# First value products in two halves of 256 queries, and one head's exponentials part by part

## The chip, the cores and the metric

The kernel runs on one core of a Trainium2 chip. Its metric is the time of one execution on the device, in microseconds (us). A core has a matrix engine (PE; its weight loads are listed as PEld), a vector engine (DVE), a scalar engine (ACT), GpSimd (POOL) and a queue engine that issues DMAs (SP). Each engine works through its own queue in order; they wait for each other through semaphores. Products of PE land in PSUM, which is used here as banks of 128 rows by 512 float32 values.

## The reference

`x` has 32 sequences of 512 tokens with 256 channels: 16 heads of 16 channels. Two causal attentions share the queries; the second one's values are the errors of the first. Then come a layer norm and, for the first sequence's 512 tokens alone, 8 experts.

```python
qk = x @ W_attn + b_attn                      # q and k; the values v are x itself, by head
y = causal_attn(q, k, v)                      # softmax(q k^T / 4), keys up to the query's own
e = v[:, :, 1:, :] - y[:, :, :-1, :]
k2 = x[:, :-1] @ W_k2 + b_k2
y2 = causal_attn(q[:, :, 1:, :], k2, e)       # a row of zeros is put in front
x = layernorm(x + proj(y) + proj(y2))
...
x = layernorm(x + experts(x))                 # experts' part: the first 512 tokens
```

## The kernel before, in words

**Groups and steps.** Four heads make a group, so a sequence has 4 groups and the whole input has 128. `step(n)` (L689) works on several groups at different stages: the row maxima of group n, the scores and exponentials of group n-1, the first attention's values of group n-2 (`a = 0`, tile `v_pad`) and the second's (`a = 1`, tile `e_pad`). The kernel is one long pipeline of such steps.

**Slots.** A step has five slots, 0 to 4. `slot(n, u)` (L395) merges four streams of products into one order for PE: for each pair of heads the maxima (`maxima`, L271, products in L301, tile `sm`) and the scores (`scores`, L356, products in L372, tile `sc`). Pair 1 begins with its scores and ends with its maxima, pair 0 the other way round. So pair 1's scores are a slot's first scores. When the last product of a stream is written down, its follow-up is written too: `exponentials()` (L380) for scores, `largest()` for maxima, which DVE does (L325).

**Scores and exponentials.** A slot's scores of one pair fill two banks, one for each head (`hh` 0 and 1). The list `banks` (L348) says what stands in a bank. Slots 1 and 4 have one part of 512 columns. Slots 0 and 2 have two, 384 and 128 columns (keys of block 1, and of block 3 of the group before). Slot 3 has two of 256. Each part takes three products (`k` = 0, 1, 2; the last subtracts the row maxima). ACT turns a bank into exponentials with one instruction of 512 columns (L384), four a slot in the order pair 1 head 0, pair 1 head 1, pair 0 head 0, pair 0 head 1. POOL then blanks the keys that lie after the query (L388).

**Banks.** `bank()` gives out four PSUM banks in turn. So whatever is the next to take a bank after a slot's four score banks takes the bank of pair 1, head 0, and must wait until its exponentials are done.

**Between the slots.** After each slot PE does what `step` listed for it (`rest`): after slot 0 a projection half (`project`, L228, tile `pj`) and an output projection (`attended`, L551, `po`); after slot 1 the first attention's values; after slot 2 transposes (`normalize`, L504, `yt`) and a projection half; after slot 3 a projection half and queries 0 to 255 of the second attention's values; after slot 4 queries 256 to 511. In the steps of the experts their products (L640, L665) are put in as well.

**Values.** `values(n, a, lo, hi)` (L428) multiplies the exponentials of key blocks `j` into one bank, for queries `lo` to `hi`, four heads to each block, and ACT copies the bank to `avs` (L450). For `a = 0` it is called once, for all 512 queries: blocks 0, 2, 1, 3 with 512, 256, 384 and 128 queries, 16 products. `gather` (L461, L462) then sends `avs` by DMA.

**Who orders what.** The order on PE, SP, DVE and POOL is the order of the program; ACT's is left to the scheduler of the language.

Of the kernel before, what the change touches and what calls it, by code (L numbers as in the profile page):

```python
# [13 lines left out]
AF = mybir.ActivationFunctionType  # L14
# [3 lines left out]
P = 128  # L18
HD = 16
# [16 lines left out]
def half(ap):  # L36
    return ap.bitcast(F32R)
# [3 lines left out]
def block_kernel(  # L41
# [16 lines left out]
    nc = tc.nc  # L58
    B, T, C = x.shape
# [21 lines left out]
    def bank(name):  # L81
        return psum.tile([P, T], F32, tag="one", name=name, bufs=4)
# [134 lines left out]
    def prepare(n):  # L217
        b, g = divmod(n, NG)
        s = seqs[b]
        heads = slice(g * GH, (g + 1) * GH)  # L220
        nc.gpsimd.tensor_copy(of_group(v_pad, g), s["x"].rearrange("p n (h d) -> p n h d", d=HD)[:, :, heads])
# [134 lines left out]
    def scores(n, u, pair):  # L356
        parts = [p for p in banks[u] if 0 <= n - p[3] < n_all]
        if not parts:
            return [], lambda: None
        ps = [bank(f"sc{n}_{u}_{pair}_{hh}") for hh in range(NH2)]  # L360
        pt = work.tile([P, NH2, T], F32, tag=f"pt{u}", name=f"pt{n}_{u}_{pair}", bufs=2)
        todo = []


        def score(d, a, j, at, k, hh, rows):
            keys = minus[a][rows] if k == 2 else d["kk"][rows, a, j * P : (j + 1) * P]
            queries = d["q"][rows, k, j * P :] if k < 2 else d["m"][rows]
            to = ps[hh][:, at * P : at * P + T - j * P]
            if k == 2:
                queries = queries.rearrange("p (r i q) -> p i r q", r=GH, i=NB)[:, j:]  # L370
                to = to.rearrange("p (i r q) -> p i r q", r=GH, q=HS)
            nc.tensor.matmul(to, half(keys), half(queries), start=(k == 0), stop=(k == 2))  # L372

        for a, j, at, lag in parts:
            d = groups[n - lag]
            d["pt", a, j, pair] = pt[:, :, at * P : at * P + T - j * P]
            for k in range(3):
                todo.append((T - j * P, partial(score, d, a, j, at, k)))

        def exponentials():  # L380
            lo = parts[0][2] * P
            hi = parts[-1][2] * P + T - parts[-1][1] * P
            for hh in range(NH2):
                nc.scalar.activation(pt[:, hh, lo:hi], ps[hh][:, lo:hi], AF.Exp, scale=HD**-0.5)  # L384

            for a, j, at, _ in parts:
                diag = pt[:, :, at * P : (at + 1) * P]
                nc.gpsimd.affine_select(  # L388
                    diag, diag, pattern=[[0, NH2], [1, P]], compare_op=ALU.is_ge, fill=0.0, base=-a,
                    channel_multiplier=-1,  # L390
                )

        return todo, exponentials
# [34 lines left out]
    def values(n, a, lo=0, hi=T):  # L428
        b, g = divmod(n, NG)
        d = groups[n]  # L430
        vals = (v_pad, e_pad)[a]

        def first_of(g, h):
            return (g // 2 * GH + h) * WIDE + 2 * (g % 2)

        ps = bank(f"av{n}_{a}_{lo}")
        order = [j for j in ([0, 2, 1, 3] if a == 0 else [0, 1, 3, 2]) if j * P < hi]
        for j in order:
            first = max(lo, j * P)
            for h in range(GH):  # L440
                nc.tensor.matmul(  # L441
                    ps[HS * h : HS * (h + 1), first - lo : hi - lo],
                    vals[:, j, first_of(g, h) : first_of(g, h) + HS],
                    d["pt", a, j, h // NH2][:, h % NH2, first - j * P : hi - j * P],
                    start=(j == order[0]),
                    stop=(j == order[-1]),
                )
        if lo == 0:
            d["avs", a] = work.tile([P, T], F32, tag="avs", name=f"avs{n}_{a}")
        nc.scalar.copy(d["avs", a][:, lo:hi], ps[:, 0 : hi - lo])  # L450

# [76 lines left out]
    def second_norm(b, t):  # L528
        norm(t, f"b{b}")
        nc.sync.dma_start(out[b].rearrange("(n p) c -> p n c", p=P), t)  # L530
# [54 lines left out]
    def store(b):  # L585
        nc.sync.dma_start(out[b].rearrange("(n p) c -> p n c", p=P), seqs.pop(b)["h"])
# [102 lines left out]
    def step(n):  # L689
        ready = lambda k: 0 <= k < n_all  # L690
        rest = [[] for _ in units]
        b, r = divmod(n, NG)
        two, odd = divmod(n, 2)
        ahead, behind = two + 1, two - 2
        if ready(n):
            prepare(n)

        def add(gap, f, *args):
            rest[gap].append(partial(f, *args))

        if ready(n - 1):
            add(0, augment, n - 1)
        if ready(2 * ahead):
            if odd:
                add(0, project, ahead, 0, T // 2)
                add(0, spread, ahead, 1, 0)
                add(2, project, ahead, 2, 0, T // 2)
                add(3, project, ahead, 2, T // 2)
            else:
                add(0, project, ahead, 1, 0, T // 2)  # L710
                add(2, project, ahead, 1, T // 2)
                add(3, project, ahead, 0, 0, T // 2)
        if ready(2 * behind) and not odd:
            add(0, narrow, behind)
        if ready(2 * two) and two and not odd:
            add(0, spread, two, 0, 1)
        if ready(n - 2):
            soon = n > n_all
            add(0 if soon else 1, values, n - 2, 0)
            add(0 if soon else 1, gather, n - 2, 0)  # L720
            rest[1 if soon else 2].insert(0, partial(normalize, n - 2))
            add(3, values, n - 2, 1, 0, T // 2)
            add(4, values, n - 2, 1, T // 2)
        if ready(2 * ahead) and odd:
            add(1, spread, ahead, 1, 1)
            add(2, spread, ahead, 0, 0)
            add(4, spread, ahead, 2, 0)
        if ready(2 * behind) and not odd:
            add(2, inverse, behind)
            add(3, unload, behind)  # L730
            add(4, widen, behind)
            if n > n_all + 1:
                add(4, weigh, behind)
                add(4, unite, behind)
        if ready(2 * behind) and odd and n < n_all + 2:
            add(1, weigh, behind)
            add(3, unite, behind)
        if ready(2 * two) and two and not odd:
            add(1, spread, two, 2, 1)
        if ready(n):  # L740
            add(4, halve, n)
        if ready(n - 2):
            add(4, gather, n - 2, 1)
        if r == 1 and b + 1 < B:
            add(2, load, b + 1)
        if r == 3 and b + 1 < B:
            add(2, load_next, b + 1)

        for b in range(B):
            end = (b + 1) * NG - 1  # L750
            last = b == B - 1
            for i in range(NB):
                if n == (end + 4 if last else min(end + 5 + i, n_all)):
                    add(0, attended, b, i)
                    if 0 < b < B - 1:
                        add(1, scaled, b, i)
            if n == end + 2:
                add(2, load_residual, b)
            for part in range(2):
                if n == (end + 3 if last else min(end + 3 + 2 * part, n_all - 1)):  # L760
                    add(3, biased, b, part)
            if 0 < b < B - 1 and n == min(end + 9, n_all + 2):
                rest[1].append(lambda b=b: store(b))


        e = n - first_expert
        if e == -1:
            rest[4] += [route, turn_tokens, lambda: load_hidden(0), lambda: load_down(0)]
        if e == 0:
            rest[0].insert(0, biases)  # L770
        if 0 <= e < E:
            rest[3].insert(0, lambda: hidden(e, 0, 0))
            rest[4].insert(0, lambda: hidden(e, 0, 1))
        if 0 <= e - 1 < E:
            rest[0].insert(0, lambda: hidden(e - 1, 1, 0))
            rest[1].insert(0, lambda: hidden(e - 1, 1, 1))
            rest[2].insert(0, lambda: down(e - 1))
            if e < E:
                rest[1].append(lambda: load_hidden(e))
                rest[2].append(lambda: load_down(e))  # L780
        if e == E:
            rest[4].append(lambda: second_norm(0, moe["acc"]))
        for s in range(len(units)):
            slot(n, s)
            for f in rest[s]:
                f()
# [94 lines left out]
```

## Time and profile before

| what | value |
|---|---|
| median of 3 runs | 2552.66 us (2551.92 to 2559.37) |
| the profiled execution's own time | 2553.1 us |
| its span in the trace | 2551.4 us |
| DVE busy | 2034.4 us (80%) |
| POOL busy | 1751.4 us (69%) |
| exponentials on ACT (L384) | 2564 instructions |
| values of the first attention on PE (L441, `v_pad`) | 4096 records, two to a product |
| values of the second attention on PE (L441, `e_pad`) | 6144 records |
| copies `avs` on ACT (L450) | 128 of 512 columns, 256 of 256 columns |

The span runs from the first to the last instruction of the program; the execution's own time has a little around it. A line of the timeline view gives the start, the length, the engine, the source line and the operation; equal instructions that follow each other are merged, with their count. Square brackets hold the engine's idle time before it and who ended it. "x32" for products of float32 means 16 products of two records.

### The profile page before, as it was taken

What the parts mean: (1) busy time and instruction counts of PE and PEld (TensorE: products, weight loads), DVE (VectorE), ACT (ScalarE), POOL (GpSimd) and SP (SyncE); (2) the same over time, 40 slices, a digit from 0 to 9 for tenths busy, and PEclk for the clock granted to TensorE, in tenths of its full rate; (3) what the DMA queues carried; (4) which work ended last, traced back from release to release, by engine and by line L of the source; (5) the groups of instructions that cost most, each with busy time, mean ns of one, the idle gap of its engine ahead of it and who ended that gap; (6) DMA issues with size and microseconds to landing.
All of it is one profiled execution on the core that took longest, in us unless ns stands there. A gap on an engine that the chain in (4) does not pass through costs nothing. (4 is left out here: it accounts for less than half of the span.)

```text
span 2551.4 us, 87424 instructions
## 1 busy us (share of the span) xinstructions
PE 2416.2 (95%) x35080; PEld 1735.8 (68%) x35080; DVE 2034.4 (80%) x3227; ACT 1660.6 (65%) x3350; POOL 1751.4 (69%) x3254
## 2 busy tenths in 40 slices
PE   7999999999999999999999999999999999999995
PEld 4766666677667667677776777677766767777763
DVE  6878777788888878888887888888887888888881
ACT  2766444476666667676766767667666667767662
POOL 4655555577777767777776777677776777777774
PEclk7999999999999999999999999999999999999997
DMA  5445433354545445445554545445454545445431
GB/s 136 109 111 134 112 100 107 96 134 125 131 133 130 120 120 129 134 131 134 132 138 106 133 125 132 132 128 139 111 132 125 135 129 134 128 115 133 127 102 60
DMA packets 262660, 314.04 MB, mean 123 GB/s; under 512 B 83064, under 2 KB 152688, under 8 KB 262256
## 3 DMA queue, kind: packets, MB, share of 16 engines
q1 hardware_dynamic: 259824, 308.01, 45.7%
q8 instruction: 278, 4.55, 0.8%
q14 instruction: 126, 1.03, 0.1%
q10 hardware_dynamic: 2368, 0.42, 0.1%
q0 software_dynamic: 64, 0.02, 0.0%
HBM read 115.26 MB, written 25.17 MB: 55 GB/s over the span
## 5 line engine op out<-in xcount | busy, mean ns | idle before, releaser
L325 DVE TENSOR_REDUCE top<-sm 128x2 f32<-128x1024 f32 (+4 forms) x1802 | 1529.4, 901 | 314.2 <-PE sc L372 189.1
L384 ACT ACTIVATE pt<-sc 128x512 f32<-128x512 f32 (+1 forms) x2564 | 1323.2, 603 | 441.2 <-PE sc L372 412.9
L388 POOL TENSOR_SCALAR_AFFINE_SELECT pt<-pt 128x256 f32<-128x256 f32 x2048 | 793.0, 409 | 636.4 <-ACT pt L384 627.4
L301 PE MATMUL sm<-kk_t,q_t 32*128 32x512 f32 (+2 forms) x7168 | 1031.1, 379 | 22.5 <-DMA kk_t<-pk 9.7
L372 PE MATMUL sc<-q_t,kk_t 32*128 32x256 f32 (+3 forms) x8192 | 993.0, 336 | 6.1 <-ACT pk L240 4.3
L372 PEld LDWEIGHTS sc<-q_t,kk_t 32*128 32x128 f32 x8192 | 646.8, 184 | 202.3 <-ACT pt L384 87.8
L372 PE MATMUL sc<-m_t,minus 32*128 32x256 f32 (+3 forms) x4096 | 694.7, 319 | 0.3
L301 PEld LDWEIGHTS sm<-kk_t,q_t 32*128 32x128 f32 x7168 | 611.1, 190 | 32.8 <-issue 18.3
L228 PE MATMUL pj<-xT,wq_sb 128*128 128x256 f32 (+1 forms) x1524 | 437.9, 411 | 44.7 <-DMA xT<-in_xT 9.3
L372 PEld LDWEIGHTS sc<-m_t,minus 32*128 32x128 f32 x4096 | 433.9, 185 | 12.4 <-issue 1.3
L228 PEld LDWEIGHTS pj<-xT,wq_sb 128*128 128x128 f32 x1524 | 264.1, 192 | 131.7 <-ACT pt L384 81.3
L441 PE MATMUL av<-pt,e_pad 128*32 128x256 f32 (+1 forms) x6144 | 335.0, 352 | 14.3 <-POOL e_pad L513 6.3
L450 ACT COPY avs<-av 128x256 f32<-128x256 f32 (+1 forms) x384 | 170.3, 444 | 265.6 <-issue 169.4
L286 PE MATMUL sm<-hide,pick 32*128 32x256 bf16 (+1 forms) x2560 | 337.0, 258 | 0.0
L441 PE MATMUL av<-pt,v_pad 128*32 128x512 f32 (+3 forms) x4096 | 303.9, 436 | 19.9 <-ACT pt L384 19.2
L441 PEld LDWEIGHTS av<-pt,e_pad 128*32 128x32 f32 x6144 | 170.0, 110 | 164.4 <-issue 46.0
L240 ACT ACTIVATE pk<-pj,bp_qk 128x256 f32<-128x256 f32 (+1 forms) x381 | 185.8, 488 | 129.5 <-PE pj L228 90.0
L441 PEld LDWEIGHTS av<-pt,v_pad 128*32 128x32 f32 x4096 | 142.0, 110 | 187.0 <-issue 160.6
L246 POOL TENSOR_TENSOR pk<-pk,lead 128x512 fp32r<-128x512 f32 x192 | 244.8, 1275 | 16.6 <-ACT lead L245 0.8
L581 POOL TENSOR_SCALAR h<-h,mv,r 128x256 f32<-128x256 f32 x120 | 147.0, 1225 | 13.1
L551 PE MATMUL po<-wp_sb,ysT 128*128 128x256 f32 x512 | 135.3, 390 | 12.7 <-POOL ysT L497 12.3
L243 POOL CAST lead<-pk 128x512 fp32r<-128x512 f32 x189 | 115.4, 611 | 28.5 <-ACT pk L240 26.8
(84 smaller groups left out, 1559.3 us busy)
## 6 DMA issues: line engine op xcount, KB each, us to landing
q_t<-lead SPq DMA_DIRECT2D x256, 128.0 KB
q_t<-pk SPq DMA_DIRECT2D x256, 128.0 KB
kk_t<-lead SPq DMA_DIRECT2D x256, 128.0 KB
kk_t<-pk SPq DMA_DIRECT2D x256, 128.0 KB
num<-avs SPq DMA_DIRECT2D x256, 128.0 KB
r<-inv SPq DMA_DIRECT2D x128, 256.0 KB
xT<-in_xT SPq DMA_DIRECT2D x32, 512.0 KB
x<-in_x SPq DMA_DIRECT2D x32, 512.0 KB
```

Source lines behind the costliest of these rows:

```text
L228: nc.tensor.matmul(ps[:, 0 : hi - lo], wq_sb[:, m, c, part * P : (part + 1) * P], seqs[b]["xT"][:, c, lo:hi], start=(c == 0), stop=(c == N ...
L240: nc.scalar.activation(pk[:, lo:hi], ps[:, 0 : hi - lo], AF.Identity, bias=bp_qk[:, m, part : part + 1])
L246: nc.gpsimd.tensor_sub(half(pk), pk, lead)
L286: nc.tensor.matmul(ps[hh][:, 0 if alone else hh].rearrange("p (k c) -> p k c", c=P)[:, first::step], pick[rows], hide[rows, kinds[0] : kin ...
L301: nc.tensor.matmul(part(ps[hh], i, na, at)[:, 0 if alone else hh], half(d["q"][rows, k, i * P : (i + 1) * P]), half(d["kk"][rows, a : a + ...
L325: nc.vector.tensor_reduce(to, view, AX.X, ALU.max)
L372: nc.tensor.matmul(to, half(keys), half(queries), start=(k == 0), stop=(k == 2))
L384: nc.scalar.activation(pt[:, hh, lo:hi], ps[hh][:, lo:hi], AF.Exp, scale=HD**-0.5)
L388: nc.gpsimd.affine_select(diag, diag, pattern=[[0, NH2], [1, P]], compare_op=ALU.is_ge, fill=0.0, base=-a, channel_multiplier=-1,)
L441: nc.tensor.matmul(ps[HS * h : HS * (h + 1), first - lo : hi - lo], vals[:, j, first_of(g, h) : first_of(g, h) + HS], d["pt", a, j, h // N ...
L450: nc.scalar.copy(d["avs", a][:, lo:hi], ps[:, 0 : hi - lo])
L581: by.tensor_scalar(t[:, i], t[:, i], mv[:, 0:1], r, ALU.subtract, ALU.mult)
```

## The change

1. The first attention's values are made in two products of 256 queries in two banks, the later half (queries 256 to 511) first. The tile `avs` is made by whichever comes first. The later half takes blocks 0, 2, 1, 3 with 256, 256, 256 and 128 queries; the earlier half takes blocks 0 and 1 with 256 and 128. ACT copies each half by itself.
2. Where a bank of pair 1's scores, a slot's first, has two parts (slots 0, 2 and 3), the exponentials of head 0 are made with one instruction for each part. Head 1, pair 0, and slots 1 and 4 stay as they were.

```diff
         def exponentials():
-            lo = parts[0][2] * P
-            hi = parts[-1][2] * P + T - parts[-1][1] * P
+            runs = [(at * P, at * P + T - j * P) for _, j, at, _ in parts]
             for hh in range(NH2):
-                nc.scalar.activation(pt[:, hh, lo:hi], ps[hh][:, lo:hi], AF.Exp, scale=HD**-0.5)
+                for lo, hi in runs if pair and not hh else [(runs[0][0], runs[-1][1])]:
+                    nc.scalar.activation(pt[:, hh, lo:hi], ps[hh][:, lo:hi], AF.Exp, scale=HD**-0.5)
...
-        if lo == 0:
+        if ("avs", a) not in d:
             d["avs", a] = work.tile([P, T], F32, tag="avs", name=f"avs{n}_{a}")
         nc.scalar.copy(d["avs", a][:, lo:hi], ps[:, 0 : hi - lo])
...
             soon = n > n_all
-            add(0 if soon else 1, values, n - 2, 0)
+            for half_of in (T // 2, 0):
+                add(0 if soon else 1, values, n - 2, 0, half_of, half_of + T // 2)
             add(0 if soon else 1, gather, n - 2, 0)
```

## The prediction

> **What bounds the kernel now.** I read the page first, then the waits, then the timeline of one step, and then counted over all steps what the timeline showed in one. The page:
>
> ```profile
> span 2551.4 us, 87424 instructions
> PE 2416.2 (95%) x35080; PEld 1735.8 (68%) x35080; DVE 2034.4 (80%) x3227; ACT 1660.6 (65%) x3350; POOL 1751.4 (69%) x3254
> L384 ACT ACTIVATE pt<-sc 128x512 f32<-128x512 f32 (+1 forms) x2564 | 1323.2, 603 | 441.2 <-PE sc L372 412.9
> ```
>
> PE is busy 95%, but ACT, at 65%, sits on the same path: its exponentials wait 412.9 us for PE's scores. The waits view has the other direction:
>
> ```profile
> PEld sc L372 <- ACT pt L384: 87.8, 244, 0.4
> PEld pj L228 <- ACT pt L384: 81.3, 229, 1.4
> PEld av L441 <- ACT pt L384: 45.8, 120, 0.9
> ```
>
> The waits are short, but there is one in almost every slot. The timeline shows what sets their length. These are slots 0, 1, 2 and 4 of one step, each with ACT's exponentials and PE's next work:
>
> ```profile
> 1207.62 2.06 ACT L384 ACTIVATE pt<-sc 128x512 f32<-128x512 f32 x4 [0.68 <-PE sc L372]
> 1208.27 0.73 PEld L228 LDWEIGHTS pj<-xT,wq_sb 128*128 128x128 f32 x4 [0.30 <-ACT pt L384]
> ...
> 1211.24 2.06 ACT L384 ACTIVATE pt<-sc 128x512 f32<-128x512 f32 x4 [1.20 <-PE sc L372]
> 1211.98 2.36 PE L441 MATMUL av<-pt,v_pad 128*32 128x512 f32 x32 [0.15 <-ACT pt L384]
> 1214.28 0.44 PE L372 MATMUL sc<-q_t,kk_t 32*128 32x384 f32 x2
> 1214.45 0.59 ACT L450 COPY avs<-av 128x512 f32<-128x512 f32 x1 [1.14 <-issue]
> 1215.46 2.06 ACT L384 ACTIVATE pt<-sc 128x512 f32<-128x512 f32 x4 [0.43 <-POOL r L578]
> 1216.11 0.66 PE L504 MATMUL yt<-ident,avs 128*128 128x128 f32 x4
> ...
> 1222.32 2.06 ACT L384 ACTIVATE pt<-sc 128x512 f32<-128x512 f32 x4 [0.50 <-PE sc L372]
> 1222.97 1.72 PE L441 MATMUL av<-pt,e_pad 128*32 128x256 f32 x32
> ```
>
> From the start of the first exponential to PE's next work it is 0.65 us in slots 0, 2 and 4 (8.27 - 7.62, 16.11 - 15.46, 22.97 - 22.32): the 0.60 us of one exponential, and 0.05 us until PE goes on, since that work takes the bank of pair 1, head 0. Read record by record over the whole trace, PE's next piece starts within 0.08 us of such an end in 98 of 116 slots 0, 119 of 120 slots 2, 115 of 116 slots 3, and 27 more in the experts' steps: 359 places. So **the first exponential of each slot ends the slot**, and its length is paid in full. A normal step takes 18.2 us.
>
> In slot 1 the time is 0.74 us, 0.09 more, in 119 of 120 steps. There the first product of values has two waits, for its bank (ACT) and for blanked exponentials (POOL), and a separate wait instruction stands ahead of it (51 ns each in the trace, PE's queue, L441). Slot 4's values have one wait and none ahead.
>
> **Part 2, the exponentials.** In the changed program ACT gets 383 more exponentials; POOL's, DVE's and SP's orders are the same to the row. The first part's exponential waits for the same count of PE as the whole did before: the last product of the bank. The second waits for nothing, and only its end reports to PE. So **nothing starts earlier**, and the split is one more instruction ahead of each release. The row: slot 2's scores of the first part end at about 15.07, its whole bank at 15.35 and the exponential starts at 15.46, the later of the two.
>
> The Trainium skill says why the bank is the unit ("PSUM — Partial Sum Buffer", section "PSUM bank collisions raise a hardware error"): PE writing and ScalarE reading one bank at once collide even at different columns, so one guards by bank. It speaks against this change; without it the first parts could start 0.28 us earlier and the sum would be some 80 us lower.
>
> Price of one more instruction: from the rows by form, 512 columns take 0.603 us and 256 take 0.392 us, so 0.181 us is fixed; the copies (0.587 and 0.372 us) give 0.157.
>
> ```profile
> L384 ACT ACTIVATE pt<-sc 128x256 f32<-128x256 f32 x8 | 2.7, 392 | 3.2 <-PE sm L286 2.0 <-PE sm L301 0.9 <-PE sc L372 0.3
> L450 ACT COPY avs<-av 128x256 f32<-128x256 f32 x256 | 95.2, 372 | 102.4 <-PE av L441 73.4 <-ACT pk L240 21.3 <-issue 7.4
> L450 ACT COPY avs<-av 128x512 f32<-128x512 f32 x128 | 75.1, 587 | 163.2 <-issue 161.9 <-PE av L441 1.2
> ```
>
> Back to back they overlap: four take 2.06, so (2.06 - 0.60) / 3 = 0.487 us from start to start, 0.116 less than one alone. The split then costs 0.041 to 0.065 us; with no overlap 0.157 to 0.181. I take 0.055, since the second part has no wait at all, fewer than the pairs that the trace shows overlapping. 359 x 0.055 = **+19.7 us**; with no overlap at 0.167, +60. Behind the split stand the three other exponentials of the slot, 0.055 later; POOL and the next slot's scores wait for those, but the scores come over 2 us later.
>
> The skill's "ScalarE: Activation LUTs", section "What ACT_TABLE_LOAD costs", gives 186 ns fixed and about 93 ns of overlap, so 93 ns a split; by that alone this term would be 33 us.
>
> **Part 1, the values.** PE gets 8 more products a step, with the same total of columns. Between the starts of the blocks of eight records, the medians over 128 steps are 0.857, 0.431, 0.645 and 0.359 us for 512, 256, 384 and 128 queries: 1.67 ns a query, but for the last, which holds the handover to the scores. The second attention's halves show 0.456, 0.432, 0.218, 0.545 and 0.456, 0.332. In the new order: 0.456 + 0.432 + 0.432 + 0.218 for the later half, 0.432 + 0.332 to 0.359 for the earlier, together 2.30 to 2.33 us against 2.292 now: +0.01 to +0.04. Were the two halves to cost what `e_pad`'s two separate ones do, 1.651 + 0.788 = 2.439, it would be +0.147. I take +0.02: the handover is paid where PE changes to scores or projections, and it doesn't between the halves.
>
> Against that, the later half's first product has only the bank's wait; the wait for POOL moves to its second and last blocks. So slot 1 should release like slot 4: **-0.09**. Together -0.07 x 120 = **-8.4 us**.
>
> ACT copies twice: 2 x 0.372 for 0.587 us, in the 1.14 us that it idles there; the first copy lies beside the earlier half. The next scores' last bank is then free about 0.2 us sooner, which is hidden behind the same slot's exponential (15.46). One more bank is taken each step; slot 2's scores then wait for pair 0's exponentials of slot 1, done by 1213.30, a microsecond before. `gather`'s DMAs are the same, issued about 0.2 us sooner.
>
> **Sum.** +19.7 - 8.4 = +11.3 on the profiled execution's 2553.1: **2564 us**. That execution was 0.4 above the median of the runs, too little to shift the number.
>
> **Rivals.**
>
> *The halves are two blocks of their own* (+0.147 instead of +0.02): 120 x 0.127 = 15 more, 2579. For it: every value product of 256 queries in the trace costs this; against it: none of those follows another at full clock.
>
> *No overlap on ACT*: 60 instead of 20, 2604. Against it: nearly all pairs of L384 overlap.
>
> *Not slower: DMA stalls shrink.* Some 60 slots are longer than their median by 0.16 to 5 us, 54 us in all, with PE short of operands that SP's queue brings; SP waits 88.2 us for `avs` copies. If the copies' 0.2 us comes through in each, that is 60 x 0.2 = 12 us less: 2552. It decides where SP's stall begins at `gather`'s wait; most begin at loads of `x`, so I think less.
>
> *The first parts start at their own products*: in slot 2 that is 15.18 instead of 15.46; the second part follows 0.38 later and ends at 15.84 instead of 16.06, 0.22 us gained in each of the 359 places, -79, and -8: 2466. The program's waits speak against it; it would take an engine that goes on before its semaphore.
>
> **How the numbers follow.** The main case has 0.62, and its own range is 2557 to 2572 (split 0.041 to 0.065, values 0 to +0.04). Separate blocks 0.10, no overlap 0.05, smaller stalls 0.15, early parts 0.03, and 0.05 for something else that is slower. The range 2551 to 2582 takes in the main case, the separate blocks and the smaller stalls, and leaves out the rest. About 0.3%, 7.7 us, is what can be told from no change: of the main case a fifth lies below 2560. Faster: 0.03 early parts, 0.04 from the stalls, 0.07. Same: 0.13 of the main case and 0.11 of the stalls, 0.24. Slower: 0.69.
>
> **What would show it.** Right: no exponential starts sooner after its slot's start (medians now 1.19 us in slots 0 and 2, 1.10 in slot 3), slots 0, 2 and 3 are each 0.04 to 0.07 longer, slot 1 0.09 shorter, the values 2.30 to 2.33. Wrong: slots that keep their length, values near 2.44, a slot 1 that still has 0.74, or split exponentials that don't overlap.

## The result, and the profile after

| | before | after |
|---|---|---|
| median of 6 runs | 2551.52 us (2547.71 to 2559.37) | 2565.49 us (2558.66 to 2579.88) |
| span of the profiled execution | 2551.4 us | 2561.5 us |
| that execution's own time | 2553.1 us | 2563.2 us |

The ratio is 1.007, 95% interval 1.0046 to 1.0093: the change made the kernel slower by 14 us in the medians and by 10 in the profiled executions. The forecast was 2564, 11 more; the interval of the ratio is 12 to 24 us, so 11 lies just below its lower end.

The page of the changed kernel:

```profile
span 2561.5 us, 92301 instructions
PE 2400.1 (94%) x37128; PEld 1762.4 (69%) x37128; DVE 2037.3 (80%) x3227; ACT 1704.5 (67%) x3861; POOL 1750.5 (68%) x3254
...
L384 ACT ACTIVATE pt<-sc 128x512 f32<-128x512 f32 (+3 forms) x2947 | 1347.2, 550 | 471.9 <-PE sc L372 451.6
```

PE has 2048 more records (two to a product, 8 products a step), and is busy 16 us less in a span that is 10 us longer: it waits more. ACT has 511 more instructions, 383 exponentials and 128 copies. The waits view of the changed kernel, in us, times and the longest:

```profile
PEld pj L228 <- ACT pt L384: 94.8, 231, 1.4
PEld sc L372 <- ACT pt L384: 88.7, 246, 0.4
PEld av L441 <- ACT pt L384: 71.1, 186, 0.9
...
PEld yt L504 <- ACT pt L384: 43.8, 120, 0.6
```

The same view of the kernel before has this for the transposes:

```profile
PEld yt L504 <- ACT pt L384: 2.5, 11, 0.4
```

The projections wait longer than before, the values more often, and the weight loads of slot 2's transposes, which hardly waited before, do so in 120 steps. PE's separate wait instructions have changed too. For the values (L441), before and after:

```profile
L441 PEldq EVENT_SEMAPHORE  x256: 51/51/51, 59.7 to 2519.0; - x128
```

```profile
L441 PEldq EVENT_SEMAPHORE  x192: 51/51/778, 59.8 to 2529.2; - x192
```

For the projections (L228), before and after, and for the transposes (L504), which had none before:

```profile
L228 PEldq EVENT_SEMAPHORE  x34: 51/51/51, 5.0 to 2376.8; - x34
```

```profile
L228 PEldq EVENT_SEMAPHORE  x236: 51/51/482, 4.7 to 2451.0; - x118
L504 PEldq EVENT_SEMAPHORE  x119: 51/51/51, 63.7 to 2500.7; - x119
```

The timeline of the changed kernel, slots 0, 1, 2 and 3 of one step, and slot 1 of the next:

```profile
1209.54 2.13 ACT L384 ACTIVATE pt<-sc 128x384 f32<-128x384 f32 x5 [0.68 <-PE sc L372]
1210.25 0.73 PEld L228 LDWEIGHTS pj<-xT,wq_sb 128*128 128x128 f32 x4 [0.36 <-ACT pt L384]
...
1213.52 2.06 ACT L384 ACTIVATE pt<-sc 128x512 f32<-128x512 f32 x4 [1.49 <-PE sc L372]
1214.17 2.37 PE L441 MATMUL av<-pt,v_pad 128*32 128x256 f32 x48 [0.39 <-ACT pt L384]
...
1217.67 1.64 ACT L384 ACTIVATE pt<-sc 128x384 f32<-128x384 f32 x4 [0.68 <-POOL r L578]
1218.38 0.66 PE L504 MATMUL yt<-ident,avs 128*128 128x128 f32 x4 [0.19 <-ACT pt L384]
...
1221.18 2.13 ACT L384 ACTIVATE pt<-sc 128x256 f32<-128x256 f32 x5 [0.67 <-PE sc L372]
1221.89 0.73 PEld L228 LDWEIGHTS pj<-xT,wq_sb 128*128 128x128 f32 x4 [0.51 <-ACT pt L384]
...
1231.99 2.07 ACT L384 ACTIVATE pt<-sc 128x512 f32<-128x512 f32 x4 [1.22 <-PE sc L372]
1232.73 2.37 PE L441 MATMUL av<-pt,v_pad 128*32 128x256 f32 x48 [0.20 <-ACT pt L384]
```

From the first exponential to PE's next work it is now 0.71 us in slots 0, 2 and 3, where it was 0.65. In slot 1 it is 0.65 in the first of the two steps and still 0.74 in the second. Over all steps, with the median length of each piece in us:

| piece | before | after |
|---|---|---|
| slot 0 | 1.842 | 1.899 |
| slot 1 | 1.797 | half of the steps 1.70 to 1.72, half as before |
| first attention's values | 2.291 | 2.301 |
| slot 2 | 1.839 | 1.902 |
| slot 3 | 1.749 | 1.799 |
| slot 4 | 1.707 | 1.704 |
| slot 0: start to the first exponential | 1.192 | 1.188 |
| slot 2: the same | 1.187 | 1.190 |

The lengths by form show what a split costs:

```profile
L384 ACT ACTIVATE pt<-sc 128x384 f32<-128x384 f32 x256 | 125.8, 491 | 187.0 <-PE sc L372 171.2 <-POOL r L578 14.9 <-POOL v_pad L221 0.9
...
L384 ACT ACTIVATE pt<-sc 128x128 f32<-128x128 f32 x256 | 69.5, 271 | 0.0
```

128 columns have no idle time ahead of them and begin 0.388 us after the 384 (median of 256 pairs), so the two end at 0.388 + 0.271 = 0.659, where one of 512 took 0.599: 0.060 more. PE goes on 0.05 us after that end, as before, though 202 more wait instructions stand ahead of L228's work and 119 ahead of L504's: all but a few of them wait for PE's own products alone, and they are over 0.68 us before the release (median).

**Ordinary and long slots.** That adds up to more than 10 us: over 110 steps (counted from slot 2 to slot 2, without the first 150 us, the experts' steps and the last 60 us) the medians times their counts give 1994.6 us before and 2014.1 after, 19.5 more. What exceeds the median of its piece by over 0.1 us fell meanwhile from 45.0 us in 66 places to 34.5 in 56, and the rest from -0.2 to -2.8 (the shorter half of slot 1 is in it): together 6 more. So in this execution a part of the cost was absorbed by long slots. It is one execution of each kernel, and the interval of the ratio, 12 to 24 us, takes in the full 19.5 as well. The experiments take up what the long slots are.

### The profile page after: what moved, and what is told of

Same layout as the page of the kernel before. It is cut to its first block, busy times and chain, and to the rows that moved or that the text cites. A ratio compares the mean times of both kernels' runs of the same rounds, so it can differ in the third digit from the quotient of the medians.

```text
span 2561.5 us, 92301 instructions
## 1 busy us (share of the span) xinstructions
PE 2400.1 (94%) x37128; PEld 1762.4 (69%) x37128; DVE 2037.3 (80%) x3227; ACT 1704.5 (67%) x3861; POOL 1750.5 (68%) x3254
## 5 line engine op out<-in xcount | busy, mean ns | idle before, releaser
L384 ACT ACTIVATE pt<-sc 128x512 f32<-128x512 f32 (+3 forms) x2947 | 1347.2, 550 | 471.9 <-PE sc L372 451.6
L372 PE MATMUL sc<-q_t,kk_t 32*128 32x384 f32 (+3 forms) x8192 | 961.3, 333 | 4.4 <-ACT pk L240 2.3
L372 PEld LDWEIGHTS sc<-q_t,kk_t 32*128 32x128 f32 x8192 | 600.7, 184 | 200.6 <-ACT pt L384 88.7
L372 PE MATMUL sc<-m_t,minus 32*128 32x256 f32 (+3 forms) x4096 | 670.3, 319 | 0.1
L228 PE MATMUL pj<-xT,wq_sb 128*128 128x256 f32 (+1 forms) x1524 | 439.0, 411 | 57.0 <-ACT pt L384 43.4
L372 PEld LDWEIGHTS sc<-m_t,minus 32*128 32x128 f32 x4096 | 390.5, 185 | 11.4 <-issue 0.2
L228 PEld LDWEIGHTS pj<-xT,wq_sb 128*128 128x128 f32 x1524 | 264.2, 192 | 145.1 <-ACT pt L384 94.8
L441 PE MATMUL av<-pt,e_pad 128*32 128x256 f32 (+1 forms) x6144 | 334.1, 351 | 14.1 <-POOL e_pad L513 6.2
L450 ACT COPY avs<-av 128x256 f32<-128x256 f32 x512 | 191.0, 373 | 209.6 <-PE av L441 103.6
L441 PE MATMUL av<-pt,v_pad 128*32 128x256 f32 (+1 forms) x6144 | 306.3, 347 | 16.6 <-ACT pt L384 11.1
L441 PEld LDWEIGHTS av<-pt,v_pad 128*32 128x32 f32 x6144 | 196.2, 110 | 130.1 <-ACT pt L384 25.7
L441 PEld LDWEIGHTS av<-pt,e_pad 128*32 128x32 f32 x6144 | 169.7, 110 | 164.1 <-ACT pt L384 45.5
```

Of the source, the lines that this page charges most:

```text
L228: nc.tensor.matmul(ps[:, 0 : hi - lo], wq_sb[:, m, c, part * P : (part + 1) * P], seqs[b]["xT"][:, c, lo:hi], start=(c == 0), stop=(c == N ...
L441: nc.tensor.matmul(ps[HS * h : HS * (h + 1), first - lo : hi - lo], vals[:, j, first_of(g, h) : first_of(g, h) + HS], d["pt", a, j, h // N ...
```

## The experiments

Theory A is the prediction's: the release of the first exponential's bank ends each slot, and a separate wait instruction that carries this release costs 0.09 us. Theory B: what counts is the work that ACT and PE get. Theory S came after the first four runs: steps with loads are paced by SP's queue, and long slots take or give back what ordinary slots gain or lose. The runs fall into three sets of four, each with its own runs of the kernel before on the same chip: median 2559.8 for the first set, 2562.8 for the second, 2560.9 for the third. Across sets the ratios to it are compared; the totals in the expectations of the first set start from 2551.5.

**1. Values in halves alone.** The change's diff without its part in `exponentials`.

> The first attention's values in two halves, the exponentials as before. Theory A (each slot ends with the release of the first exponential's bank, and a separate wait instruction that carries this release costs 0.09 us more): slot 1 is 0.09 shorter in the half of the steps in which the first product has one wait, 60 x 0.09 = 5.4 less, and the values take 0.01 longer, 1.2 more: some 4 us less than before, 2547. Theory B (what counts is the work that an engine gets): 8 products and one copy more a step, 0.157 us on ACT, 120 x 0.157 = 19 more, 2570.

Measured: 2564.1, ratio 1.0018 (1.0001 to 1.0035), 5 us slower (0 to 9). The ordinary pieces do what theory A says: slot 1 is 1.704 in half of the steps and 1.80 in the others, the values take 2.301. But long slots exceed by 58.0 us in 89 places instead of 45.0 in 66. Neither theory's sum holds: A's gain is there in the slots and gone in the total; B's 19 is not there either.

**2. Exponentials by parts alone.** The change's part in `exponentials` only.

> The exponentials of head 0 part by part, the values as before. Theory A: the first release comes 0.06 later in slots 0 and 2 and 0.05 in slot 3, in 359 places: 20 us more, 2571, with no slot's first exponential earlier. Theory B (work of ACT): 383 instructions with 0.055 more each, 21 more; it gives the same here, and is told apart by the next run. If the first parts start at their own products, 79 less.

Measured: 2565.5, ratio 1.0031 (1.0012 to 1.0050), 8 more (3 to 13) and not 20. The ordinary slots again have the full cost: slots 0, 2 and 3 are 1.899, 1.904 and 1.800. In slots 0 and 2 no first exponential begins earlier (1.188 and 1.192); in slot 3 it is 0.010 sooner.

**3. Head 1 split instead of head 0.**

```diff
-                for lo, hi in runs if pair and not hh else [(runs[0][0], runs[-1][1])]:
+                for lo, hi in runs if pair and hh else [(runs[0][0], runs[-1][1])]:
```

> As the run before, but head 1's exponentials are split and head 0's are whole: the same number of instructions, and the first release is not touched. Theory A: slots 0 and 3 keep their length; in slot 2 the projection that follows the transposes takes the second bank, whose release now comes 0.06 later with 0.016 to spare, so up to 0.045 x 120 = 5 more, 2551 to 2557. Theory B: 20 more, 2571.

Measured: 2566.6, ratio 1.0026 (1.0006 to 1.0046), 7 more (2 to 12): theory A's 5 lies in it and theory B's 20 does not. In the pieces it is theory A alone: slots 0 and 2 stay at 1.841 and 1.843, slot 3 at 1.743, and from the transposes to the projection after slot 2 it is 0.550 instead of 0.493, 0.057 more where up to 0.045 was worked out. The total by itself decides little, since run 2 came out at 8, where both theories had 20.

**4. Two tiles for v_pad.** The first run, with

```diff
-    v_pad = const.tile([P, NB, NG // 2 * GH * WIDE + 1], F32, name="v_pad")
+    v_pad = [const.tile([P, NB, GH * WIDE + 1], F32, name=f"v_pad{i}") for i in range(NG // 2)]
...
-        vals = (v_pad, e_pad)[a]
+        vals = (v_pad[g // 2], e_pad)[a]
```

> As the first run, and the values' tile v_pad is two tiles, one for each pair of groups, so that the later half's first product has no wait for POOL in any step. Theory A: slot 1 is 0.09 shorter in all steps, 120 x 0.09 = 10.8 less, the values 0.01 longer: some 10 us less than before, 2542. Theory B: as the first run, 19 more.

Measured: 2569.6, ratio 1.0034 (1.0014 to 1.0054). Slot 1 is now 1.710 at the median, short in nearly all steps, and yet the total has the largest median of the four: slot 3 is 0.022 longer at the median (1.771), and long slots exceed by 65.3 us in 90 places. A gain of 0.09 in each step thus ends as a loss. That needs a second bound, in the long slots.

**What the long slots wait for.** Of every four steps (one sequence) two hold most of them: 18.77 and 18.92 us on average in the kernel before, against 18.20 and 18.44. They are the steps behind those in whose last slots SP issues the loads: `xs` (L213 to L215) ahead of the one, `xT` and `x` (L94, L207) ahead of the other. Where the trace names a cause, PE's largest gap lies ahead of a product that reads `kk_t`, `q_t` or `m_t`, ahead of a projection that waits for `xT` (11 places), or behind ACT's `pk`, which waits until `q_t<-pk` has been sent: all of it work of SP's queue. That queue in the kernel before, by the timeline:

```profile
1220.47 0.60 SPq L213 DMA_DIRECT2D xs<-in_x  x1
1221.11 0.38 SPq L214 DMA_DIRECT2D xs<-in_x  x1
1221.54 3.20 SPq L215 DMA_DIRECT2D xs<-in_x  x1
1224.84 0.48 SPq L259 DMA_DIRECT2D kk_t<-lead  x1
```

L215 loads a single row of 1 KB into one partition, and its issue holds the queue for 2.93 us (median of 32; 90.9 us in all), five times as long as the 384 KB of L213. What stands behind it in the queue is issued that much later. The trace's DMA packets show more: in 29 of 32 cases the 127 rows of L214 go out one after another, 0.042 us apart, the last one 8.4 us after L214's issue (median), and in 30 of 32 L215's hold ends when 115 to 127 of the 128 rows of L214 and L215 have still to start. So the 127 rows ahead of it may be what holds the single row.

**5 to 8. One load in place of three**, in the kernel before, in the changed kernel, and in runs 1 and 4. The row in question is used by no result; here it comes from the next sequence, so that 128 rows go in one piece (the last sequence keeps the three loads).

```diff
+        if b + 1 < B:
+            rows = x.rearrange("b t c -> (b t) c")[b * T + 1 : b * T + T + 1]
+            nc.sync.dma_start(s["xs"], rows.rearrange("(n p) c -> p n c", p=P))
+            return
```

> The kernel before, with the shifted rows xs of a sequence loaded by one DMA in place of three (the last row, which no result uses, comes from the next sequence). In the traces so far the third of these DMAs, of one row, holds SP's queue 2.9 us in each of 32 sequences. Theory S (beside the releases, SP's queue paces the steps with loads, and long slots are PE's waiting for what SP brings late): the long slots' excess, 45 us in 109 steps before, falls by half or more, 25 us less, with ordinary slots unchanged. Theory A alone (only releases count): no change within 3 us.

Measured: 2511.6, ratio 0.9816 (0.9790 to 0.9842): 51 us less in the medians, 47 by the ratio, twice what was expected. Ordinary slots are unchanged (1.842, 1.797, 1.838, 1.749, 1.706), long slots exceed by 6.4 us in 11 places instead of 45.0 in 66. SP's own waits, in the waits view, before and with the single load:

```profile
SPq L346 <- DMA turned<-tr: 367.4, 117, 6.1
SPq L483 <- DMA inv<-den: 129.7, 64, 4.1
SPq L338 <- DVE tr L336: 111.3, 56, 9.4
```

```profile
SPq L342 <- DVE tr L340: 295.3, 126, 13.5
SPq L465 <- ACT avs L454: 148.0, 75, 10.7
SPq L350 <- DMA turned<-tr: 143.0, 93, 3.6
```

(L338 and L346 of before are L342 and L350 here.) Before, SP came late to `turned` (it waited for DVE in 56 steps only) and then stood through the DMA's way to memory and back; now it is ready and waits for DVE in 126. So the three loads of `xs` made most of the long slots, which fits theory S. The gain is 51 / 31 = 1.6 us for each merged load, less than the hold of 2.9. The run takes away the single row and the 127 slow rows together, and no run parts the hold of SP's queue from the rows that are still on their way behind it; nor was it followed how `xs` lengthens the step behind `xT`, two steps later.

> The changed kernel with the same single load. Theory S: the change's full cost in ordinary slots shows once the long slots no longer absorb part of it, +22 against the run before (0.17 to 0.20 a step x 128), so about as slow as the kernel before. Theory A alone: as the changed kernel.

Measured: 2532.0, ratio 0.9895 (0.9869 to 0.9920), 20.4 more than run 5 on the same chip. With the long slots nearly gone (6.2 us), this is what the change costs when little absorbs it.

> Only the values in halves, with the single load. Theory S: 4 us less than the kernel before with the single load, the gain that was given back in long slots. Theory A alone: 4 us less than before. If the halves cost by themselves (theory B), some 5 to 19 more than with the single load alone.

Measured: 2512.0, 0.4 more than run 5, ratio 0.9816 (0.9791 to 0.9841). The halves are worth nothing either way, within the scatter of these runs (2511.0 to 2513.6). In the profiled executions the 106 steps behind the experts' are 1.0 us shorter than in run 5, where some 3 were due by the pieces, and the steps of the experts take 0.7 more.

> The values in halves, v_pad in two tiles, with the single load. Theory S: 10 us less than the kernel before with the single load, some 35 less than before, the fastest so far. Theory B: slower than the single load alone by 8, as the fourth run was than before.

Measured: 2508.1, ratio 0.9804 (0.9779 to 0.9830), 3.5 less than run 5 and the fastest of all, ahead of both kernels. Slot 1 is 1.707 in nearly all steps, 10.8 us by itself, less 1.2 for the values; but slot 2 is 0.007 and slot 3 0.011 longer at the median, with the first exponential that much later after the slot's start, and this gives back 2.2. Where the other 4 went wasn't settled.

**9. Parts alone, with the single load.**

> Only the exponentials of head 0 part by part, with the single load of xs, compared with the kernel before with that single load (2511.6). Theory A (the first release ends the slot): 0.06 in slots 0 and 2 and 0.05 in slot 3, 20 more, 2532, all of the changed kernel's difference there. Theory B (work of ACT): 21 more too.

Measured: 2535.8, ratio 0.9899 (0.9881 to 0.9918). Against run 5's ratio that is 0.0083, 21 us (24 in the medians of the two chips). The whole of the changed kernel's cost sits in this part.

**10. Head 1 split, with the single load.**

> As the run before, but head 1's exponentials are split and head 0's are whole; compared with 2511.6. Theory A: slots keep their length, only the projection after slot 2's transposes waits for the second bank, 0.057 x 120 = 7 more, 2518. Theory B: 20 more, 2532.

Measured: 2522.7, ratio 0.9847 (0.9827 to 0.9866): 8 us by the ratios, 11 by the medians. With as many more instructions on ACT as run 9 has, it costs 13 us less than run 9, on the same chip. The transposes' piece is 0.550, all slots are as before. Theory B, 20 for both, falls.

**11. Four parts.** The condition also asks for more than one part in the bank, so slots 1 and 4 stay whole.

```diff
-            runs = [(at * P, at * P + T - j * P) for _, j, at, _ in parts]
+            runs = [(at * P + i, at * P + i + P) for _, j, at, _ in parts for i in range(0, T - j * P, P)]
```

> Head 0's exponentials in slots 0, 2 and 3 in four parts of 128 columns, compared with 2511.6. From the trace of the changed kernel, 0.157 from start to start for 128 columns and 0.271 alone: 3 x 0.157 + 0.271 = 0.742 for 0.599, 0.143 more. Theory A: 359 x 0.143 = 51 more, 2563. If a split cost nothing beyond the first, as 2532; if each extra instruction cost the 0.17 that it takes alone, 359 x 0.51 = 183 more, 2695.

Measured: 2583.3, ratio 1.0082 (1.0064 to 1.0100): 68 us by the ratios against 51 expected. Slots 0, 2 and 3 are 2.027, 2.028 and 1.932, 0.183 to 0.190 longer each and not 0.143. The timeline shows the release behind four parts, 0.83 us after the start (0.65 whole, 0.71 in two):

```profile
1204.33 2.26 ACT L388 ACTIVATE pt<-sc 128x128 f32<-128x128 f32 x7 [0.68 <-PE sc L376]
1205.16 0.73 PEld L232 LDWEIGHTS pj<-xT,wq_sb 128*128 128x128 f32 x4 [0.49 <-ACT pt L388]
```

From start to start the parts are 0.158 apart, as expected; but the later ones of a row last longer (up to 0.299, where 0.269 is the shortest), so each further part costs 0.06 and the sum of the expectation is too small.

**12. The earlier half first.**

```diff
-            for half_of in (T // 2, 0):
+            for half_of in (0, T // 2):
```

> The values in halves with the earlier half first, exponentials whole, compared with 2511.6 and with the later half first (2512.0). Theory A: the first product now waits for POOL in every step, so slot 1 keeps 1.797 in all of them and the values are 0.01 longer: 1 us more than 2511.6; with the later half first the shorter slot 1 of half of the steps should have given 4 less than that. If the order does not matter, the same as 2512.0 in the slots too.

Measured: 2514.8, ratio 0.9822 (0.9803 to 0.9841); the interval spans both expectations. The pieces decide: slot 1 is 1.798 in all steps (1.796 already at the tenth percentile), where run 7 has 1.72 there; the values take 2.301 in both. So the order matters, through the wait, by 0.09 in half of the steps.

## Why the prediction was right, and where it was not

*The first release ends the slot.* Right. PE's next piece begins within 0.08 us of it in 99% of slots 2 and 3 in the changed kernel too, and run 10 against run 9 shows that the place of an instruction counts and not its work.

*Nothing starts earlier.* Right: 1.188 us after the start of slot 0 for 1.192, 1.190 for 1.187 in slot 2; in slot 3 it is 0.010 sooner, 1.088 for 1.098. This is the guard by bank that the Trainium skill asks for ("PSUM — Partial Sum Buffer", section "PSUM bank collisions raise a hardware error"); what happens without it wasn't tried.

*+19.7 for the split.* Right in size: 0.060 us at the release for the 0.055 that was taken, 0.057, 0.063 and 0.050 in the lengths of slots 0, 2 and 3; 20 to 24 us in runs 6 and 9. The estimate of 93 ns a split from the figures of the Trainium skill ("ScalarE: Activation LUTs", section "What ACT_TABLE_LOAD costs") would have given 33; here the measurement decides.

*+0.01 to +0.04 for the halves.* Right, 2.301 for 2.291. The rival with two separate blocks, 2.44, falls: the handover is paid once.

*-0.09 in slot 1 in all steps.* This term was mis-sized. PE's wait instructions of L441 fell from 256 to 192, by 64 and not by 128, and slot 1 is short in 61 of 120 steps. I read that the wait for POOL's blanking moves to later blocks, and missed a second wait for POOL, for the copy of `x` into `v_pad` (L221). Of every four groups the last two keep it. `v_pad` holds both pairs' columns side by side for each key block, so the copy for one pair and the columns of the other interleave; with two tiles (run 4) the wait is gone from the program. The term is -0.09 x 61 = -5.5 and +0.01 x 120 = +1.2, -4 instead of -8.4.

*Smaller stalls.* I gave this rival 12 us and 0.15, for a reason that is not the one: the long slots did shrink, by 10.5 us in 110 steps of the profiled execution, but not because `gather` can go out sooner (the second copy ends 2.81 us after the first product's start, for 3.06 before): run 1 has the same halves with ordinary slots that are not longer, and there they grew by 13. They are smaller where ordinary slots are longer, in the changed kernel and in run 2 (37.5 us), about as before in run 3 (46.8), and larger where slot 1 is shorter, in runs 1 and 4. That longer slots leave SP's queue more time fits this, but each figure is from one execution, and it isn't shown beyond that.

So that 2564 was met is in part luck. Almost without long slots the change costs 20 (runs 5 and 6), 9 more than the sum's 11. Of these 9, 4 are the wait that stayed in half of the steps; the other 5 stay open: in the totals the halves don't even gain the 4 that are left to them (run 7 against 5: 0.4 more). Against the 9 stand some 6 to 10 that long slots seem to have absorbed and that the sum leaves out. A slip that changed nothing: by its own terms the main case's range ends at 2570, not 2572.

## What to carry to other kernels

Find the event that ends each stage in almost every pass (here one exponential's end, +0.05 us), and price an edit by what it does to that event: an instruction split ahead of it cost 20 us in all, the same split one place further back 8 to 11. A small gain in the ordinary passes shows in the total only if no second bound fills the gap, so count ordinary and long passes apart; the long ones led here to three loads, and making them one was worth over three times what the change cost. When a wait is said to be gone, look at the built program for every group, not for one.

## What the runs showed of the hardware

- The issue of a DMA of one row of 1 KB into one partition, right behind one of 127 rows, held SP's queue for 2.93 us (1.73 to 3.70, 32 of them); the issue of the 127 rows took 0.39 and of the 384 ahead of them 0.59. The 127 rows went out one after another, 0.042 us apart, in 29 of 32 cases. Three loads in one made the kernel 1.8% faster. Whether the single row or the 127 ahead of it make the hold stays open.
- A wait instruction of its own ahead of a product, when it is the one that ends last, costs PE 0.09 us more than the same wait held by the product (0.145 for 0.053 from the exponential's end), though it is listed with 0.051. Where the separate wait is over before the release (L228 and L504 in the changed kernel), PE goes on after 0.052 as without it.
- Exponentials from PSUM in a row begin 0.157, 0.264, 0.388 and 0.478 us apart, after one of 128, 256, 384 and 512 columns (0.281 between the two of 256 of one bank), and last 0.271, 0.384, 0.491 and 0.599 us each. In a row the later ones last longer: of 512 columns 0.592 us as the second and 0.655 as the seventh (run 11).
